# A convolution chain with a Haar shrinkage layer: 25 instead of 21 of 64 final convolutions of three images put off, ScalarE forming 8 instead of 6 of 16 products, and the stores of these convolutions issued from another queue

## The chip, the core and the metric

The kernel runs on one core of one Trainium2 chip. The time is the device time of one execution in microseconds (us). Before the change it was 2994.05 us, the median of three runs (2990.19, 2994.05 and 2999.53). All arithmetic is in 32-bit floating point.

## The reference: what is computed

The input x holds B = 4 images of C = 64 channels, each channel a plane of 256 x 256 numbers. Four layers are applied in sequence.

```python
def conv(x, hx, hy, bias):            # layers 0, 1 and 3, each with its own filter
    k = hx[:, None] * hy[None, :]      # per channel: an outer product of two filters of length 256
    y = irfft2(rfft2(x, 512) * rfft2(k, 512) / 512)[:256, :256]
    return y + x * bias                # a causal 2D convolution plus a skip

def shrinkage(x, v, conv_w, tau):      # layer 2
    f1 = haar2d(x)                     # all levels, along both axes
    for i in range(2):
        f4 = einsum("bchw,oc->bohw", f1 * v[i], conv_w[i])   # channels are mixed
        acc += sign(f4) * relu(abs(f4) - tau[i])
    return haar2d(acc, inverse=True) + x
```

The filters hx and hy come from small networks with sines, computed once per layer. Because a filter is an outer product, the convolution of one plane is two products with triangular Toeplitz matrices, one for the rows and one for the columns.

## The kernel before: how the work is tiled and staged

**One convolution of one plane** is two calls of `contract` (lines 187 to 190), named `first` and `second`. A contract is four matmuls of TensorE: the plane's tile is the stationary operand, a Toeplitz tile `t` read from the padded filter is the moving one, with 256 columns on line 189 and 128 columns on line 190. The result comes out transposed, so two contracts restore the layout. After the first, ScalarE copies the result from PSUM to SBUF (line 198, tile `a`); after the second, VectorE adds the skip (line 211, tile `y`). In a profile the PSUM results are `pa` and `py`. Every fp32 matmul stands there as two records.

**The stages.** Layers 0 and 1 of a batch element run in `convolutions(b)`, which goes on to the Haar transform of the rows and columns (tiles `sd`, `sp`, `pz`, `co`) and stores `keep` and `coef` in DRAM. Then `mixing(b)` takes 64 groups g: four matmuls per group (line 334, result `px`, 128 x 1024 in two PSUM banks, two such results at a time), the product with `v` (lines 351 and 353), absolute value and sign on ScalarE (359, 360), the threshold and the signed product on VectorE (361, 366) and a sum into `z` (370). The 16 strips of 64 columns of the product with `v` are divided: VectorE does 16 - n_act of them in one instruction (line 351), ScalarE does n_act of them in n_act instructions (line 353), which wait for VectorE's. At last `inverse(b)` takes the 64 channels: per channel a strided copy of `z` (387), the inverse Haar along the rows (`pw`, 394 and 395), a rounded part and a remainder (397, 398), the columns (`pu`, 407), three VectorE instructions that form the plane `u` (411, 414, 415), and then layer 3's convolution of that plane and its store (`last`, lines 430 to 435).

**What is put off.** Mixing of image b runs beside the convolutions of image b + 1. The last mixing, of image 3, has none beside it. So layer 3's convolutions of some channels of images 0, 1 and 2 (`put_off`, line 455: the channels 2, 5, ..., 62, 21 of 64) are not done in `inverse`: the plane `u` is stored in DRAM (`late`, line 425) and is loaded again during the last mixing by `convolution` (lines 437 to 448), which spreads all 63 of them evenly over that mixing's ticks. Each of these loads a plane (`v`, tag "in", three buffers), loads a Toeplitz tile (tag "toep", five buffers), and runs `first`, `second` and the store of the result (tag "co", two buffers).

**Order.** Every stage is entered in a list with a tick and a place (`at`), the list is sorted, and the program is built in that order (lines 488 and 489); the compiler then arranges the instructions of each engine, still in one fixed order per engine, by costs of its own. Each engine works through its list in order and waits where a semaphore asks it to. A DMA issued by SyncE or by ScalarE likewise stands in that engine's list. `spread` (line 451) gives the ticks: 63 convolutions over 71 ticks, so at most one begins in a tick.

Of the kernel before, what the change touches and what calls it, by code (L numbers as in the profile page):

```python
# [16 lines left out]
B, C, S, EMB, ORD = 4, 64, 256, 33, 64  # L17
P = 128
# [19 lines left out]
def conv_seq_kernel(ctx, tc, x, fz, fw, bias, decay, haar, haar_row, factors, vt, taut, wmix, out):  # L38
# [14 lines left out]
    nc = tc.nc  # L53
# [123 lines left out]
    def toeplitz(layer, c, name):  # L177

        t = tp.tile([P, 2, S], F32, name=name, tag="toep")
        nc.sync.dma_start(t, ap(pads[layer], c * 2 * ROW, [[1, P], [ROW, 2], [1, S]]))  # L180
        return t
# [34 lines left out]
    def butterfly(b):  # L216

        d = mx.tile([P, 2, C], F32, name=f"bfly_{b}", tag="mag")
        nc.vector.tensor_sub(d, z[:, :, 0, :], z[:, :, 1, :])
        nc.vector.tensor_add(z[:, :, 0, :], z[:, :, 0, :], z[:, :, 1, :])  # L220
        nc.vector.tensor_copy(z[:, :, 1, :], d)
# [5 lines left out]
    def at(tick, place, run, unit):  # L227
        events.append((tick, place, len(events), run, unit))
# [81 lines left out]
    def mixing(b, start, n_act):  # L310

        st = {}

        def load(g):
            f = mx.tile([P, 2, S], F32, name=f"f_{b}_{g}", tag="f", bufs=3)
            nc.sync.dma_start(f, coef[b].rearrange("k c p w -> (k c) p w")[:, 2 * g : 2 * g + 2])
            st[g] = {"f": f}
            if g % GT == 0:
                t = mx.tile([P, 2, GT, 16], F32, name=f"vt_{b}_{g}", tag="vt")
                nc.sync.dma_start(t, scales[g // GT])  # L320
                st["vt", g // GT] = t

        def scale(g, i):
            return st["vt", g // GT][:, i, g % GT, :]

        def over(g, i, n):
            return scale(g, i)[:, :n].unsqueeze(2).to_broadcast([P, n, C])

        def mix(g):
            f = st[g]["f"]  # L330
            ps = psx.tile([P, 2, 2, S], F32, name=f"px_{b}_{g}", tag="mix")
            for q in range(2):
                for h in range(2):
                    nc.tensor.matmul(  # L334
                        ps[:, h, q, :],
                        f[:, q, h * P : (h + 1) * P],
                        wb.rearrange("p r n -> p (r n)"),
                        start=True,
                        stop=True,
                    )  # L340
            if g == 0:

                one, two = ps[:, :, 0, :P], ps[:, :, 0, P:]
                d = mx.tile([P, 2, P], F32, name=f"d_{b}", tag="mag")
                nc.vector.tensor_copy(d, two)
                nc.vector.tensor_sub(two, one, d)
                nc.vector.tensor_add(one, one, d)
            f4 = mx.tile([P, 16, C], F32, name=f"f4_{b}_{g}", tag="f4")
            px = ps.rearrange("p h q (r i o) -> p (h q r i) o", r=2, i=2)
            n = 16 - n_act  # L350
            nc.vector.tensor_tensor(f4[:, :n], px[:, :n], over(g, 0, n), ALU.mult)  # L351
            for j in range(n, 16):
                nc.scalar.mul(f4[:, j], px[:, j], scale(g, 0)[:, j : j + 1])  # L353
            st[g]["f4"] = f4

        def shrink(g):
            f4 = st[g]["f4"]
            mag = mx.tile([P, 16, C], F32, name=f"mag_{b}_{g}", tag="mag")
            nc.scalar.activation(mag, f4, AF.Abs)  # L359
            nc.scalar.activation(f4, f4, AF.Sign)  # L360
            nc.vector.tensor_sub(mag, mag, over(g, 1, 16))  # L361
            st[g]["mag"] = mag

        def signed(g):
            mag = st[g]["mag"]
            nc.vector.scalar_tensor_tensor(mag, mag, 0.0, st[g]["f4"], ALU.max, ALU.mult)  # L366

        def add(g):
            parts = st.pop(g)["mag"].rearrange("p (h r i) o -> p h r i o", h=2, i=2)
            nc.vector.tensor_add(z[:, :, 4 * g : 4 * g + 4, :], parts[:, :, :, 0, :], parts[:, :, :, 1, :])  # L370

        for g in range(S // 4):
            at(start + g - 2, 0, load, g)
            for s, stage in enumerate([mix, shrink, signed, add]):
                at(start + g + s, -1 - s, stage, g)

    def inverse(b, start, put_off):

        st = {}

        def fetch(c):
            if c == 0:
                butterfly(b)
            r = mx.tile([P, 2, 2, P], F32, name=f"r_{b}_{c}", tag="f", bufs=3)
            nc.sync.dma_start(r, keep[b][c])
            a = mx.tile([P, 2, 2, P], F32, name=f"zc_{b}_{c}", tag="mag")
            nc.scalar.copy(a, z[:, :, :, c].rearrange("p h (i k) -> p h k i", k=2))  # L387
            st[c] = {"r": r, "z": a}

        def rows(c):  # L390
            a = st[c]["z"]
            ps = psm.tile([P, 2, 2, P], F32, name=f"pw_{b}_{c}", tag="mm")
            for m in range(2):
                nc.tensor.matmul(ps[:, m, 0, :], a[:, 0, m, :], hsinv, start=True, stop=True)  # L394
                nc.tensor.transpose(ps[:, m, 1, :], a[:, 1, m, :], ident)  # L395
            w = mx.tile([P, 2, 2, 2, P], F32R, name=f"w_{b}_{c}", tag="f4")
            nc.scalar.copy(w[:, 0], ps)  # L397
            nc.vector.tensor_tensor(w[:, 1], ps, w[:, 0].bitcast(F32), ALU.subtract)
            st[c]["w"] = w
            if c not in put_off:  # L400
                st[c][2] = toeplitz(2, c, f"t2_{b}_{c}")

        def cols(c):
            ps = psm.tile([P, 2, 2, P], F32, name=f"pu_{b}_{c}", tag="mm")
            flat = "p m e w -> p (m e w)"
            for i in range(2):
                nc.tensor.matmul(  # L407
                    ps.rearrange(flat), hb, st[c]["w"][:, i].rearrange(flat), start=(i == 0), stop=(i == 1)
                )
            t = io.tile([P, 2, 2, P], F32, name=f"t_{b}_{c}", tag="res", bufs=BUFS["res"])  # L410
            nc.vector.scalar_tensor_tensor(t, st[c]["r"], 0.5, ps, ALU.mult, ALU.add)  # L411
            u = io.tile([P, 2, S], F32, name=f"u_{b}_{c}", tag="y", bufs=BUFS["y"])
            v = u.rearrange("p m (w e) -> p m w e", e=2)
            nc.vector.tensor_add(v[:, :, :, 0], t[:, :, 0, :], t[:, :, 1, :])
            nc.vector.tensor_sub(v[:, :, :, 1], t[:, :, 0, :], t[:, :, 1, :])
            st[c]["u"] = u

        ends = last(b, st)
        for c in range(C):

            at(start + c, -1, fetch, c)
            at(start + c + 1, -9, rows, c)
            at(start + c + 2, -8, cols, c)
            if c in put_off:
                at(start + c + 3, -5, lambda c: nc.scalar.dma_start(late[b, c], st.pop(c)["u"]), c)
            else:
                for s, stage in enumerate(ends):
                    at(start + c + 3 + s, s - 7, stage, c)

    def last(b, st):  # L430
        return [
            first(b, st, "u", 2, "a3"),
            second(b, st, "a3", 2, "u", "y3", "co"),
            lambda c: nc.scalar.dma_start(out[b, c].rearrange("(k p) w -> p k w", p=P), st.pop(c)["y3"]),
        ]

    def convolution(which, ticks):

        for (b, c), tick in zip(which, ticks):
            st = {}  # L440

            def load(c, b=b, st=st):
                u = io.tile([P, 2, S], F32, name=f"v_{b}_{c}", tag="in", bufs=3)
                nc.sync.dma_start(u, late[b, c])
                st[c] = {"u": u, 2: toeplitz(2, c, f"t2_{b}_{c}")}

            for s, stage in enumerate([load, *last(b, st)]):
                at(tick + s, -s, stage, c)


# [1 line left out]
        return [begin + i * (end - begin - 1) // (n - 1) for i in range(n)]  # L452


    put_off = range(2, C, 3)

    one, two, three = filters(0, nc.scalar), filters(1, nc.scalar), filters(2, nc.sync)
    one[0]()
# [14 lines left out]
    ahead = C  # L473
    start = ready + 3
    for b in range(B):
        mixing(b, start, 12 if b + 1 < B else 6)
        end = start + groups + 3
        if b + 1 < B:
            ready = convolutions(b + 1, spread(ahead, end + 2), in_parts=range(0, C, 2 if b == 0 else 1), border=end)
        else:  # L480
            convolution(
                [(i, c) for i in range(B - 1) for c in sorted(put_off)], spread(start - 2, end + 2, (B - 1) * len(put_off))
            )
        inverse(b, end, put_off if b + 1 < B else ())

        start = max(end + C, ready + 3)
        ahead = start - 3
# [111 lines left out]
```

## Time and profile before

| What | Value |
|---|---|
| median of three runs | 2994.05 us |
| the profiled execution, its own time | 2994.63 us |
| its span, first to last instruction | 2992.8 us |
| TensorE clock granted | 1.000 of full |
| TensorE matmul busy | 2929.2 us, 98% of the span |
| TensorE weight loads busy | 2610.1 us, 87% |
| VectorE busy | 2535.0 us, 85% |
| ScalarE busy | 2147.1 us, 72% |
| DMA, read and written in HBM | 426.77 MB and 219.48 MB |

The stages follow from the first and the last `px` matmul of each mixing, in microseconds from the start of the span:

| Stage | from | to | length |
|---|---|---|---|
| filters, tables, layers 0 and 1 of image 0 | 0 | 457.5 | 457.5 |
| mixing 0 / inverse 0 | 457.5 / 867.4 | 867.4 / 1099.7 | 409.9 / 232.3 |
| mixing 1 / inverse 1 | 1099.7 / 1543.0 | 1543.0 / 1779.4 | 443.3 / 236.4 |
| mixing 2 / inverse 2 | 1779.4 / 2222.3 | 2222.3 / 2455.75 | 442.9 / 233.45 |
| mixing 3 / inverse 3 | 2455.75 / 2728.5 | 2728.5 / 2992.8 | 272.75 / 264.3 |

An engine's busy time is the union of the times of its instructions. A mean duration of an instruction is longer than the distance from its start to the next start where instructions overlap, so where work is added up below, distances of starts are used. PE is TensorE's matmul, PEld its weight load, DVE is VectorE, ACT is ScalarE, SP is SyncE.

### The profile page before, as it was taken

The numbers are of one execution on the slowest core, as the hardware profiler recorded it, in microseconds if no ns is written. First come the engines' busy times: TensorE is split into PE (matmuls) and PEld (weight loads), VectorE is DVE, ScalarE is ACT, GpSimd is POOL, SyncE is SP. The second block draws the span as 40 slices with busy tenths as digits, with TensorE's granted clock in tenths as the row PEclk, the third lists the DMA queues.
The fourth block names the chain that finished last, engine by engine and source line by source line (L and its number), as shares of the span: only waits on it lengthen the run. The fifth ranks groups of instructions, "written<-read, shape, count | busy, mean of one in ns | idle before, by whom it ended". The sixth has DMA issues, their size and how long they took to land. (4 is left out here: it accounts for less than half of the span.)

```text
span 2992.8 us, 51867 instructions
## 1 busy us (share of the span) xinstructions
PE 2929.2 (98%) x16950; PEld 2610.1 (87%) x16950; DVE 2535.0 (85%) x4544; ACT 2147.1 (72%) x4973; POOL 0.2 (0%) x4
## 2 busy tenths in 40 slices
PE   7999999999999999999999999999999999999999
PEld 6899988888888888888888988888888988888998
DVE  4766778999988879999989879999998889998776
ACT  1333337989876658889886658989886768887554
POOL 0000000000000000000000000000000000000000
PEclk9999999999999999999999999999999999999999
DMA  5877776676667876666677876676677887777776
GB/s 146 250 233 230 229 232 207 206 206 199 204 196 245 247 216 202 206 210 201 207 212 241 253 222 198 209 212 202 205 210 234 254 239 229 229 233 220 211 212 186
DMA packets 562496, 649.72 MB, mean 217 GB/s; under 512 B 44369, under 2 KB 447412, under 8 KB 562100
## 3 DMA queue, kind: packets, MB, share of 16 engines
q1 hardware_dynamic: 446132, 494.94, 57.9%
q10 hardware_dynamic: 116096, 151.46, 14.1%
q8 instruction: 137, 2.24, 0.3%
q14 instruction: 131, 1.07, 0.1%
HBM read 426.77 MB, written 219.48 MB: 216 GB/s over the span
## 5 line engine op out<-in xcount | busy, mean ns | idle before, releaser
L189 PE MATMUL py<-t,a 128*128 128x256 f32 x3072 | 923.1, 382 | 19.2 <-ACT a L198 12.3
L198 ACT COPY a<-pa 128x512 f32<-128x512 f32 x768 | 472.4, 617 | 440.6 <-PE pa L190 305.7
L190 PEld LDWEIGHTS py<-t,a 128*128 128x128 f32 x3072 | 583.4, 190 | 79.3
L353 ACT ACTIVATE f<-px,vt 128x64 f32<-128x64 f32 x2688 | 588.8, 351 | 87.7 <-DVE f L351 81.8
L190 PE MATMUL py<-t,a 128*128 128x128 f32 x3072 | 590.1, 274 | 0.0
L189 PEld LDWEIGHTS py<-t,a 128*128 128x128 f32 x3072 | 491.0, 191 | 78.2 <-ACT a L198 35.7
L334 PE MATMUL px<-wb,f 128*128 128x256 f32 x2048 | 503.5, 381 | 16.7 <-ACT f L353 16.7
L334 PEld LDWEIGHTS px<-wb,f 128*128 128x128 f32 x2048 | 362.6, 191 | 62.1 <-ACT f L353 26.7
L361 DVE TENSOR_TENSOR mag<-mag,vt 128x1024 f32<-128x1024 f32 x256 | 312.2, 1220 | 30.9 <-ACT mag L359 28.8
L366 DVE SCALAR_TENSOR_TENSOR mag<-mag,f 128x1024 f32<-128x1024 f32 x256 | 311.9, 1218 | 3.8 <-DVE sd L267 0.3
L397 ACT CAST w<-pw 128x512 fp32r<-128x512 f32 x256 | 150.4, 587 | 227.9 <-PE pw L395 215.1
L189 PE MATMUL pa<-t,y 128*128 128x256 f32 x1024 | 306.9, 382 | 1.7 <-DVE y L211 1.4
L189 PE MATMUL pa<-t,x 128*128 128x256 f32 x1024 | 305.6, 380 | 1.3 <-issue 1.3
L359 ACT ACTIVATE mag<-f 128x1024 f32<-128x1024 f32 x256 | 284.3, 1110 | 18.7 <-DVE z L370 6.8
L387 ACT COPY zc<-z 128x512 f32<-128x512 f32 x256 | 282.4, 1103 | 2.0 <-ACT w L397 0.8
L360 ACT ACTIVATE f<-f 128x1024 f32<-128x1024 f32 x256 | 274.0, 1070 | 12.1 <-DVE sd L266 5.9
L211 DVE SCALAR_TENSOR_TENSOR y<-x,bsb,py 128x512 f32<-128x512 f32 x256 | 190.3, 743 | 57.8 <-PE py L190 49.9
L189 PE MATMUL pa<-t,u 128*128 128x256 f32 x772 | 232.8, 383 | 3.2 <-PE pu L407 3.2
L411 DVE SCALAR_TENSOR_TENSOR t<-r,pu 128x512 f32<-128x512 f32 x256 | 175.1, 684 | 64.1 <-PE pu L407 60.6
L278 DVE TENSOR_TENSOR sp<-sd,sp 128x512 fp32r<-128x512 f32 x224 | 153.9, 687 | 83.0 <-ACT sp L277 81.3
L190 PEld LDWEIGHTS pa<-t,x 128*128 128x128 f32 x1024 | 194.6, 190 | 26.3
L190 PEld LDWEIGHTS pa<-t,y 128*128 128x128 f32 x1024 | 194.5, 190 | 26.3
(67 smaller groups left out, 4449.0 us busy)
## 6 DMA issues: line engine op xcount, KB each, us to landing
t<-pad SPq DMA_DIRECT2D x768, 256.0 KB, 4.0
x<-in_x SPq DMA_DIRECT2D x256, 256.0 KB, 3.9
keep<-sd ACTq DMA_DIRECT2D x256, 256.0 KB, 3.0
coef<-co SPq DMA_DIRECT2D x256, 256.0 KB, 3.2
f<-coef SPq DMA_DIRECT2D x256, 256.0 KB, 4.0
r<-keep SPq DMA_DIRECT2D x256, 256.0 KB, 3.3
out_y<-y ACTq DMA_DIRECT2D x256, 256.0 KB, 3.7
late<-u ACTq DMA_DIRECT2D x63, 256.0 KB, 2.7
```

What stands on the lines that cost most here:

```text
L189: nc.tensor.matmul(ps[:, m, :], src[:, 0, m * P : (m + 1) * P], t[:, ::-1], start=True, stop=False)
L190: nc.tensor.matmul(ps[:, m, P:], src[:, 1, m * P : (m + 1) * P], t[:, : P - 1 : -1], start=False, stop=True)
L198: nc.scalar.copy(a, ps)
L211: nc.vector.scalar_tensor_tensor(y, s[res], bsb[:, layer, c : c + 1], ps, ALU.mult, ALU.add)
L334: nc.tensor.matmul(ps[:, h, q, :], f[:, q, h * P : (h + 1) * P], wb.rearrange("p r n -> p (r n)"), start=True, stop=True,)
L353: nc.scalar.mul(f4[:, j], px[:, j], scale(g, 0)[:, j : j + 1])
L359: nc.scalar.activation(mag, f4, AF.Abs)
L360: nc.scalar.activation(f4, f4, AF.Sign)
L361: nc.vector.tensor_sub(mag, mag, over(g, 1, 16))
L366: nc.vector.scalar_tensor_tensor(mag, mag, 0.0, st[g]["f4"], ALU.max, ALU.mult)
L387: nc.scalar.copy(a, z[:, :, :, c].rearrange("p h (i k) -> p h k i", k=2))
L411: nc.vector.scalar_tensor_tensor(t, st[c]["r"], 0.5, ps, ALU.mult, ALU.add)
```

## The change

Three things change together. `put_off` becomes the channels c with c mod 5 equal to 2 or 4: 25 of 64, 75 in the three images instead of 63. They are spread over the same 71 ticks, so that in four ticks two begin. In the last mixing n_act is 8 instead of 6, so that VectorE's instruction has 512 columns instead of 640 and ScalarE has eight strips instead of six. The stores of the put-off convolutions' results are issued by SyncE instead of ScalarE; the stores of all other results stay on ScalarE.

```diff
-        ends = last(b, st)
+        ends = last(b, st, nc.scalar)
...
-    def last(b, st):
+    def last(b, st, queue):
         return [
             first(b, st, "u", 2, "a3"),
             second(b, st, "a3", 2, "u", "y3", "co"),
-            lambda c: nc.scalar.dma_start(out[b, c].rearrange("(k p) w -> p k w", p=P), st.pop(c)["y3"]),
+            lambda c: queue.dma_start(out[b, c].rearrange("(k p) w -> p k w", p=P), st.pop(c)["y3"]),
         ]
...
-            for s, stage in enumerate([load, *last(b, st)]):
+            for s, stage in enumerate([load, *last(b, st, nc.sync)]):
                 at(tick + s, -s, stage, c)
...
-    put_off = range(2, C, 3)
+    put_off = [c for c in range(C) if c % 5 in (2, 4)]
...
-        mixing(b, start, 12 if b + 1 < B else 6)
+        mixing(b, start, 12 if b + 1 < B else 8)
```

## The prediction

> **What bounds the kernel now.** I read the windows by stage first (the table of stages, from the first and last `px`), then the timeline of a saturated stretch for the pace of each matmul, then the groups and the waits of the last mixing, because that is where the moved work goes. The windows' columns are stretch, length, busy time and count of PE, PEld, DVE, ACT and POOL, granted clock, DMA share and GB/s; the rows are mixing 1, mixing 3, inverse 1 and inverse 2.
>
> ```profile
> 1099.70:1543.00 443.30, 434.92 (x2422) 386.76 (x2420) 408.52 (x713) 387.98 (x1091) 0.00 (x0) 1.00 0.68 206
> 2455.75:2728.50 272.75, 267.96 (x1436) 235.98 (x1435) 265.65 (x311) 233.98 (x553) 0.00 (x0) 1.00 0.79 232
> 1543.00:1779.40 236.40, 234.04 (x1470) 210.88 (x1470) 199.17 (x393) 156.09 (x234) 0.00 (x0) 1.00 0.78 238
> 2222.30:2455.75 233.45, 230.46 (x1445) 207.40 (x1445) 198.47 (x392) 155.50 (x232) 0.00 (x0) 1.00 0.78 239
> ```
>
> TensorE is at 98 to 99% in all of them. In mixing 3 VectorE stands beside it at 265.65 of 272.75 us (97%; 92% in mixing 1), ScalarE at 86% (88%).
>
> Busy time hides small stretches, so I take the pace from starts. In the timeline of the last inverse the engine never waits:
>
> ```profile
> 2802.08 0.39 PE L394 MATMUL pw<-hrow,zc 128*128 128x128 f32 x2
> ...
> 2803.21 0.59 PE L189 MATMUL pa<-t,u 128*128 128x256 f32 x2
> ...
> 2804.51 0.60 PE L189 MATMUL py<-t,a 128*128 128x256 f32 x2
> ...
> 2805.82 0.39 PE L394 MATMUL pw<-hrow,zc 128*128 128x128 f32 x2
> ```
>
> A channel's `pw` and `pu` take 1.13 us, a contract 1.31 (2803.21 to 2804.51, and to 2805.82), a convolution 2.62. The four `px` of a group take 1.73 (eight records from 2602.95 to 2604.68).
>
> With these, mixing 3 is 64 x 1.73 = 110.7 us, plus 115 contracts (460 records of line 189, four each) x 1.31 = 150.7, plus 0.5 for a `pu`: 261.9 of work in 272.75. So **10.8 us are lost, 4.1% of the work**. Mixing 1: 226 contracts 296.1, `px` 110.7, 49 split `pz` at 0.47 (0.55 from start to start, less 0.08 by which the record before is shorter) 23.0, `pu` 0.5: 430.3 of 443.3, lost 13.0 or 3.0%. Mixing 2 has the same work in 442.9: 2.9%.
>
> Who is late in mixing 3, from the waits in that stretch (total, times, longest):
>
> ```profile
> ACT f L353 <- DVE f L351: 14.5, 18, 1.8
> PEld px L334 <- ACT f L353: 6.7, 12, 1.2
> PEld py L189 <- ACT a L198: 5.8, 17, 0.8
> DVE y L211 <- DMA out_y<-y: 1.6, 2, 0.9
> ```
>
> The chain is VectorE's part of the product with `v`, then ScalarE's, then `px` gets its banks back. VectorE at 97% starts it.
>
> **What the Trainium skill says.** "Perfetto Trace Analysis", section "Identifying the Most-Contended Engine", warns that matmul busy time is no measure of the distance to the limit, and names the weight loads' share. The trace agrees: matmul 98% in both, weight loads 86.5% in mixing 3, but 203.06 of 220 us (92%) in the stretch of the last inverse without waits. "ScalarE: Activation LUTs", section "What ACT_TABLE_LOAD costs", gives about 280 ns + 0.833 ns per column for an activation with one operand per partition, 333 ns at 64 columns as an estimate, with overlap back to back. The row of line 353 shows 326 ns, and six end after 1.33 us, so a further one costs (1.33 - 0.33) / 5 = 0.20; I use 0.20. "DMA: Bandwidth & Descriptors", section "Issuing engines are not separate DMA queues": another issuer saves only issue time. The trace shows that time on ScalarE's queue as 0.42 us (2612.45), inside a sign instruction that runs from 2612.14 to 2613.20.
>
> **The change, part by part.**
>
> *Twelve more convolutions put off.* Nothing is saved: 12 x 2.62 = 31.4 us of TensorE move. The order of the changed program, which is fixed once it is built, has 8, 8 and 6 contracts fewer between the mixings (22 x 1.31 = 28.8 us), 20 more from the first `px` to the last in mixing 3 (26.2) and 2 more behind it (2.6). The sum is zero, so the result hangs on lost time alone. The extra 12 stores and 12 loads of 256 KB use DMA: mixing 3 moves per group 272 KB for `px` and now 75/70 x 768 KB for convolutions, 1.10 MB in about 4.6 us, 240 GB/s; the page shows slices of 253 and 254 without such waits, so I take zero.
>
> *In the three inverses* per channel remain 1.13 us and 2 x 0.6 contracts instead of 2 x 0.667. VectorE loses only eight `y` (each 0.66 from start to start) there: in inverse 1 it goes from 199.2 of 236.4 us (84%) to about 193.9 of 225.9 (86%). TensorE stays the bound. I add 0.3 us to each for less slack, 1 in all; bounds are -1 (less to wait for) and +2 each.
>
> *Eight products instead of six* in mixing 3. VectorE: line 351 takes 818 ns at 640 columns and 420 at 256 (the row of mixing 0), 1.04 ns per column, so 128 fewer save 0.13 us per group. Its distances of starts in one group (from line 351 at 2604.27: 0.73, 1.14, 0.60, 1.14 behind it, and 0.66 per `y`) make 3.61 + 0.9 x 0.66 = 4.20 us now, and 3.48 + 1.07 x 0.66 = 4.19 after. ScalarE: six strips to the absolute value 1.41, that 0.97, copy 0.46, sign 0.96 (2609.30 on) make about 3.75; after, 1.81 + 0.97 + 0.96 + 1.07 x 0.46 = 4.23. TensorE: from 261.9 / 64 = 4.09 to 1.73 + 135 x 1.31 / 64 = 4.50. So VectorE, at 4.20 in a group of 4.26 now, comes to 4.19 under a TensorE of 4.50 (93%), ScalarE to 94%.
>
> *Stores from SyncE.* Removed from ScalarE: no busy time, as above. Added to SyncE: 75 issues of 0.38 us, in a queue with some 1.3 us of issues per group. The new wait, for `y`, has the next loads behind it. In the changed order the store of convolution k stands directly ahead of the `v` load of k + 3, whose buffer (three of them) is freed by that same `y`, so it waits no longer than before; then come `f` and `t`, used one or more groups later. With a landing of 3.7 to 4.0 us that hides. If that cover goes, in the four ticks with two convolutions, it costs up to 1.5 us each. The two waits for `out_y` (1.6 us on VectorE) may go; worth nothing while TensorE is the bound. Bounds: -1.6 and +6; value 0.
>
> **The sum.** Mixing 3 after: 110.7 + 135 x 1.31 + 0.5 = 288.1 us of work. Its balance is then that of mixing 1 (VectorE 93, ScalarE 94 against 92 and 88), so I take mixing 1's loss, 3.0%: 8.6, in all 296.7, +23.9. Inverses -28.8 + 1.0, last inverse +2.6. Total -1.3 us. Behind the last `px` five convolutions follow each other in both orders, and TensorE waits for the copy in each (2731.52, 2735.08, 2738.64: 3.56 apart instead of 2.62), so that loss stays. The profiled execution, 2994.63 (span 2992.8 and 1.8 around it), becomes 2993.3; the median of the runs lies 0.6 below it: **2993 us**.
>
> **The rivals.**
>
> *Faster.* VectorE's pressure is the whole loss, and once it has slack mixing 3 loses 0.5%, 1.4 us: 288.1 + 1.4 - 272.75 - 28.8 + 2.6 = -9.4, 2985 or below. For it: the longest chain of waits begins at VectorE. Against: mixings 1 and 2, with VectorE at 92%, still lose 3%.
>
> *A new wait on SyncE's queue.* The stores hold back loads in the four double ticks, +6 us: 2999. For it: `v` has one conv's slack less there. Against: no wait of TensorE for a load stands among those of mixing 3 now.
>
> *Slower: the copy comes late.* With ScalarE at 94%, `a` (line 198), which stands between `pa` and `py`, is queued behind eight strips or an absolute value. From the end of `pa` (2734.24) to `py` (2735.08) an undelayed copy takes 0.84 us; two `px` between them cover 0.87, three 1.30. In the changed order 17 of 60 such gaps hold two, against 9 of 54, and 27 hold three against 22. Delays beyond 0.03 us in the former and 0.46 in the latter reach TensorE: 0.4 us in each of the 44 is 18 us, plus the 2 to 3 that remain otherwise, 20 (7%) where 10.8 were: +9 on -26.2 + 26.2, and with 1 to 2 in the inverses 3005. It decides once ScalarE's group passes TensorE's 4.50, that is above 0.23 us per strip. Against: trains of 12 in mixing 1 run while it loses 3%.
>
> **How the numbers follow.** My forecast 0.55, the SyncE wait 0.07, faster 0.12, slower 0.26. A measurement of this kernel tells about 0.3% (9 us) from no change, so the first two count as the same: 0.62. Range: low from a loss of 1.5% in mixing 3 (-4.3) and 1 us less in each inverse (-4), with the stores' 1.6: 2983; high from a loss of 8% (+14) and 1 us in each inverse (3 instead of the 1 that I took, +2): 3009. It leaves the ends of the outer cases out.
>
> **What would show it.** Mixing 3 about 297 us, the inverses 222, 226 and 226; VectorE below 94% and ScalarE at 91 to 94% of mixing 3; waits of `px` for line 353 smaller, of `py` for line 198 about as now. I am wrong if mixing 3 passes 303 us with `py` waiting for the copy over 12 us, or if the inverses shorten by less than 7 us each.

## The result and the profile after

| | median | range | ratio to the kernel before, 95% |
|---|---|---|---|
| before | 2994.06 us | 2990.19 to 2999.53, 20 runs | |
| after | 2999.82 us | 2995.23 to 3003.28, 20 runs | 1.0020 [1.0014, 1.0027] |

The change costs 5.8 us, where I forecast a gain of 1.3. That is inside the 0.3% that I had called about no change; with twenty runs on each side the interval excludes it. The profiled execution of after took 3002.87 us (span 3001.1), 3 us above its median; the one of before had a span of 2992.8, so the two traces differ by 8.3.

| stage | before | after | forecast | difference to forecast |
|---|---|---|---|---|
| head | 457.5 | 458.8 | 457.5 | +1.3 |
| mixings 0, 1, 2 | 409.9, 443.3, 442.9 | 409.6, 443.4, 443.3 | the same | +0.2 |
| inverses 0, 1, 2 | 232.3, 236.4, 233.5 | 224.2, 228.1, 227.2 | 27.8 less in all | +5.1 |
| mixing 3 | 272.8 | 298.8 | 296.7 | +2.1 |
| last inverse | 264.3 | 267.8 | 2.6 more | +0.9 |

The head's 1.3 says nothing: in traces of kernels with the same head it lies between 455.9 and 461. The inverses gave back 22.7 us instead of 27.8, and mixing 3 grew by 26.0 instead of 23.9. With the forecast's -1.3 the traces miss it by 9.6 us: 5.1 in the three inverses, 2.1 in mixing 3, 0.9 in the last inverse, and the rest in the head and the other mixings.

The windows of after, in the columns and the order of the prediction (stretch, length, busy time and count of PE, PEld, DVE, ACT, POOL, clock, DMA share, GB/s; mixing 1, mixing 3, inverse 1, inverse 2):

```profile
1092.52:1535.96 443.44, 435.43 (x2422) 386.79 (x2420) 408.75 (x713) 387.19 (x1091) 0.00 (x0) 1.00 0.69 206
2434.57:2733.33 298.76, 297.85 (x1596) 255.33 (x1595) 275.64 (x324) 263.77 (x697) 0.00 (x0) 1.00 0.79 241
1535.96:1764.11 228.15, 224.03 (x1406) 201.03 (x1406) 195.58 (x389) 155.22 (x230) 0.00 (x0) 1.00 0.80 242
2207.38:2434.57 227.19, 222.89 (x1398) 199.90 (x1398) 195.68 (x389) 155.11 (x230) 0.00 (x0) 1.00 0.79 241
```

In mixing 3 TensorE is 99.7% busy, against 98.2% before. Read alone, that says the stage is perfect. But its work by starts is 288.1 us, so 10.7 of 298.8 are lost, as many as the 10.8 before. The weight loads' share hints at it: 85.5% (86.5% before), where a stretch without waits had 92%. VectorE fell from 97 to 92%, as forecast; ScalarE is at 88%, not 91 to 94.

The pace of the matmuls has not changed. From the timeline of after in the last inverse (start, duration), a channel from `pw` to `pw` is 3.74 us: 1.13, 1.30 and 1.31.

```profile
2802.80 0.39 PE L394 MATMUL pw<-hrow,zc 128*128 128x128 f32 x2
...
2803.93 0.59 PE L189 MATMUL pa<-t,u 128*128 128x256 f32 x2
...
2805.23 0.60 PE L189 MATMUL py<-t,a 128*128 128x256 f32 x2
...
2806.54 0.39 PE L394 MATMUL pw<-hrow,zc 128*128 128x128 f32 x2
```

Who waits in mixing 3 of after (total us, times, longest):

```profile
ACT a L198 <- PE pa L190: 21.6, 14, 3.8
PEld py L189 <- ACT a L198: 14.2, 55, 0.8
ACT f L353 <- DVE f L351: 11.9, 7, 2.9
...
PEld px L334 <- ACT f L353: 4.8, 12, 0.6
...
DVE y L211 <- DMA out_y<-y: 3.0, 2, 2.5
...
PEld pa L189 <- DMA v<-late: 0.4, 1, 0.4
```

ScalarE waited for VectorE before (14.5); now it waits longest for TensorE's `pa`, and TensorE's `py` waits for ScalarE's copy, 55 times instead of 17. Loads of planes, which would show a blocked SyncE queue, cost 0.4 us on the weight loads. Against the matmuls' usual distances TensorE loses 4.4 us behind those late weight loads of `py`, 3.2 between two `px`, 2.4 between a `px` and a `py`. In the trace of before the same count gives 1.6 behind late weight loads of `py`, 2.6 between two `px`, 1.8 between a `px` and a `py`, and 5.1 between a `pa` and a `px`. So the wait for the `px` banks, which the prediction blamed, did shrink (from 7.7 to 3.2 us), and the wait for the copy grew by as much (from 3.4 to 6.8).

### The profile page after: what moved, and what is told of

It is laid out like the page before. It is cut to its first block, busy times and chain, and to the rows that moved or that the text cites. A ratio compares the mean times of both kernels' runs of the same rounds, so it can differ in the third digit from the quotient of the medians.

```text
span 3001.1 us, 51988 instructions
## 1 busy us (share of the span) xinstructions
PE 2935.7 (98%) x16950; PEld 2605.3 (87%) x16950; DVE 2533.6 (84%) x4544; ACT 2169.3 (72%) x5101; POOL 0.2 (0%) x4
## 5 line engine op out<-in xcount | busy, mean ns | idle before, releaser
L353 ACT ACTIVATE f<-px,vt 128x64 f32<-128x64 f32 x2816 | 615.6, 352 | 83.0 <-DVE f L351 82.6
L359 ACT ACTIVATE mag<-f 128x1024 f32<-128x1024 f32 x256 | 287.7, 1124 | 10.7 <-DVE f L351 6.4
L189 PE MATMUL pa<-t,u 128*128 128x256 f32 x724 | 218.6, 384 | 6.3 <-PE pu L407 5.0
```

What stands on the lines that cost most here:

```text
L189: nc.tensor.matmul(ps[:, m, :], src[:, 0, m * P : (m + 1) * P], t[:, ::-1], start=True, stop=False)
```

## The experiments

**Theories.** *Order*: the change makes the compiler lay out other instruction lists, and in mixing 3 the lists of TensorE and ScalarE fit each other worse, whatever the queue of the stores costs by itself. *Queue*: SyncE's stores hold back the loads behind them. *Copy*: ScalarE with eight strips is simply too full. For the inverses: *held buffer* (a put-off plane's `u`, tag "y" with three buffers, can't be reused until its store has landed) against *cover* (too little TensorE work per channel for VectorE's chain).

### Each edit alone, and two of the three

```diff
# put25_only: on the kernel before
+    put_off = [c for c in range(C) if c % 5 in (2, 4)]
# act8_only: on the kernel before
+        mixing(b, start, 12 if b + 1 < B else 8)
# sync_only: on the kernel before, with `last` taking its queue as in the change
+            for s, stage in enumerate([load, *last(b, st, nc.sync)]):
# after_act_queue: on the kernel after
-            for s, stage in enumerate([load, *last(b, st, nc.sync)]):
+            for s, stage in enumerate([load, *last(b, st, nc.scalar)]):
```

> Only the 25 of 64 channels are put off; six strips on ScalarE, stores on ScalarE as before. If the loss comes from the inverses (cover theory: less TensorE work per channel over VectorE's chain), the three inverses come to about 224, 228 and 227 us as in the changed kernel, and the time is 3000 or more: mixing 3 has VectorE at about 4.32 us per group under TensorE's 4.50, so its loss is 10 to 14 us and its length 298 to 302. If the loss came from the eight strips or the queue of the stores, the inverses would be 222, 226 and 226 and the time 2992 to 2995.

> Only eight strips instead of six in the last mixing, 21 channels put off. Cover theory: the inverses stay at 232, 236 and 233 us; mixing 3 falls from 272.75 by 2 to 4 us, since VectorE gets 0.13 us per group back and 10.8 us are lost there; time 2990 to 2992. Rival (ScalarE with eight strips delays the copy between pa and py): mixing 3 gets 2 us longer or more, time 2996 or above.

> Only the stores of the put-off convolutions go to the sync engine. All theories but one: no change, 2994 within 2 us, mixing 3 at 272 to 273. If stores on the sync queue hold loads back, mixing 3 gets 2 to 6 us longer with waits of pa for v.

> The changed kernel, but with its put-off stores issued by ScalarE. Cover theory: the same as the changed kernel, 3000 within 2 us, inverses 224, 228 and 227. If the stores' queue matters in the last mixing, the difference to 3000 is over 3 us, either way.

| | median | ratio | mixing 3 | inverses 0, 1, 2 |
|---|---|---|---|---|
| put25_only | 3000.82 | 1.0025 [1.0015, 1.0036] | 296.0 | 224.8, 228.2, 229.1 |
| act8_only | 3011.65 | 1.0063 [1.0049, 1.0076] | 287.7 | 232.1, 236.3, 232.1 |
| sync_only | 2999.99 | 1.0018 [1.0011, 1.0025] | 277.9 | 232.3, 236.0, 232.0 |
| after_act_queue | 2997.67 | 1.0013 [1.0006, 1.0019] | 292.6 | 224.6, 229.0, 226.0 |

Every edit alone costs, and the parts don't add: 6.3, 17.2 and 5.5 us by medians alone, 5.8 together. The shortfall of the inverses comes with the 25 planes and with nothing else. In mixing 3 eight strips are worst where they stand alone. The waits of act8_only there:

```profile
PEld px L334 <- ACT f L353: 20.6, 16, 2.7
...
PE px L334 <- ACT f L353: 15.6, 7, 2.3
```

Seven waits of some 2.2 us: at seven places TensorE's list asks for a `px` whose banks ScalarE has not yet read. VectorE had been relieved, and the stage got longer. Not all of it is waiting. The granted clock of this stretch was 0.97, and in all five runs that of the whole execution was 0.997 or 0.998; the trace has five stretches of 3.4 us at half clock, each beginning within 0.7 us of the end of one of the seven waits:

```profile
2537.58 1.69 PE L334 MATMUL px<-wb,f 128*128 128x256 f32 x4 [2.22 <-ACT f L353]
2539.07 1.06 PE L189 MATMUL py<-t,a 128*128 128x256 f32 x2
...
2541.53 0.60 PE L189 MATMUL pa<-t,v 128*128 128x256 f32 x2
```

The pair of matmuls that takes 0.60 us elsewhere took 1.06. Of 27.2 us lost in this stage (287.7 less 260.5 of work) 15.6 are the seven waits, and about 8.5 (half of five times 3.4) are the slower clock. So the 17.2 us hold both.

sync_only has another sort of place: in nine convolutions `py` follows its `pa` directly, with nothing in between to cover the copy.

```profile
PE py L189 <- ACT a L198: 7.1, 14, 0.7
```

The edit only names another queue, yet mixing 3 is 5.2 us longer, and the lists of TensorE, ScalarE and VectorE are others: the kernel before has no such adjacent pair in this stretch. That speaks for *order*, and I pinned orders next.

### TensorE's order alone

A pinned kernel adds dependencies without semaphores between successive instructions of one engine, which fix their order; the traces show the lists in the order given.

```diff
+    for earlier, later in zip(queue, queue[1:]):   # TensorE's matmuls of the last mixing
+        tc.add_manual_dep(later, earlier.name, <no semaphore>)
```

> The changed kernel, stores on the sync queue, but TensorE's order from the first to the last px of the last mixing is pinned to the order that the compiler chose when ScalarE issued the stores (45 gaps between pa and py with four px, instead of 27 with three and 14 with two). Order theory (the queue acts only through the order that the compiler picks): mixing 3 at 292 to 294 us, py waits for its copy a few times instead of 55, time 2996 to 2998. Queue theory (the stores on the sync queue themselves delay something): mixing 3 stays at 298 to 299 and the time at 2999 to 3001.

> The kernel before, stores on ScalarE, with TensorE's order in the last mixing pinned to the one that the compiler chose with the stores on the sync queue (nine gaps between pa and py with nothing in them). Order theory: nine waits of 0.84 us for the copy, mixing 3 at 277 to 279 us, time 2998 to 3001. Queue theory: mixing 3 at 272 to 274, time 2994 to 2995.

after_pinned: 3001.23 us, 1.0021 [1.0014, 1.0029], mixing 3 295.5. before_pinned: 3008.05, 1.0044 [1.0031, 1.0056], mixing 3 286.4 instead of the 277.9 of the kernel whose order it took. Neither settled it. TensorE's list is only half of a pair: with ScalarE's list left as the compiler made it, `py` of before_pinned waited 25.4 us for copies (32 times, on the weight loads).

### All three engines' orders: the queue and the order apart

Now the lists of TensorE, ScalarE and VectorE in mixing 3 (254, 315 and 323 steps) are held to those of after_act_queue, with the stores on SyncE; and then the converse.

```diff
+    for order in ORDERS:               # TensorE, ScalarE, VectorE
+        ...
+            tc.add_manual_dep(later, earlier.name, <no semaphore>)
```

> The changed kernel, stores on SyncE, but with the order of TensorE, ScalarE and VectorE in the last mixing held to that of the version whose stores are on ScalarE's queue, 254, 315 and 323 steps; only the queue of the stores then differs from that version. If the queue matters only through the orders that the compiler made from it: last mixing 292 to 294 us, and about 2997.7. If waits in SyncE's queue, or later loads, are the cost: last mixing 297 to 300, and about 3000 or more.

> The converse: stores on ScalarE's queue, but the three engines' orders in the last mixing held to the changed kernel's. If the order is the cause and the queue is not: last mixing near or above the changed kernel's 298.8 us (299 to 302), about 3002. If the queue has a part of its own that is worth more than 3 us: last mixing 292 to 296, about 2998.

In each field stand mixing 3, its sum with the last inverse, and the median of the whole kernel. The sum is the fairer one, since after's order has 135 contracts ahead of the last `px` and the other 134 (1596 and 1588 records, eight to a contract), with the odd one done behind it.

| | stores on SyncE | stores on ScalarE |
|---|---|---|
| after's order | 298.8; 566.5; 2999.82 | 303.3; 569.4; 3005.73 |
| after_act_queue's order | 289.7; 558.2; 2993.50 | 292.6; 562.9; 2997.67 |

The pinned ones have ratios of 0.9996 [0.9988, 1.0004] (after_all_pinned) and 1.0040 [1.0028, 1.0053]. Down the columns, by the sums, after's order costs 8.3 and 6.5 us (6.3 and 8.1 by medians). Along the rows SyncE's queue *gains* 2.9 and 4.7 (5.9 and 4.2). In each row and each column one kernel is pinned and the other has the compiler's own lists. What pinning does by itself was not run; it enters with opposite signs, so that it drops out of the means, if it adds the same everywhere: 7.4 us for the order and 3.8 for the queue. The change lost the queue's gain to the lists that came with it. This settles *queue* against *order*: both kernels of a column have the same queue.

The window and the waits of mixing 3 of after_all_pinned, where the added lines have moved the numbers (line 353 is 415, 351 is 413, 198 is 255, 189 is 244, 334 is 394, 359 is 422, 360 is 423):

```profile
2433.64:2723.34 289.70, 288.62 (x1588) 258.16 (x1586) 269.46 (x322) 259.96 (x696) 0.00 (x0) 1.00 0.80 247
```

```profile
ACT f L415 <- DVE f L413: 24.1, 56, 2.3
DVE y L270 <- PE py L246: 6.4, 8, 1.6
ACT a L255 <- PE pa L246: 5.9, 4, 3.8
...
PEld px L394 <- ACT f L415: 3.4, 8, 0.6
...
PEld py L244 <- ACT a L255: 0.8, 1, 0.8
```

`py` waits once instead of 55 times. ScalarE's wait for VectorE has doubled, 24.1 us, and costs TensorE next to nothing, since it stands where TensorE has other work: the stage loses 2.9 us in all. The weight loads are at 89.1%, and on 286.8 us of work (134 contracts) the stage loses 2.9, 1.0%. That speaks against *copy* too: the same eight strips per group, with ScalarE busy for 89.7% of the stage, need not cost more.

The two orders, seen in ScalarE's timeline. First after:

```profile
2616.76 1.06 ACT L360 ACTIVATE f<-f 128x1024 f32<-128x1024 f32 x1
2619.17 0.59 ACT L198 COPY a<-pa 128x512 f32<-128x512 f32 x1 [1.36 <-PE pa L190]
2619.66 1.75 ACT L353 ACTIVATE f<-px,vt 128x64 f32<-128x64 f32 x8
```

Then after_all_pinned, one group of it:

```profile
2617.28 0.31 ACT L415 ACTIVATE f<-px,vt 128x64 f32<-128x64 f32 x1 [0.87 <-DVE f L413]
2617.49 1.05 ACT L423 ACTIVATE f<-f 128x1024 f32<-128x1024 f32 x1
2618.43 1.53 ACT L415 ACTIVATE f<-px,vt 128x64 f32<-128x64 f32 x7
2619.81 0.63 ACT L255 COPY a<-pa 128x512 f32<-128x512 f32 x1
```

In after the copy stands ahead of the eight strips here: ScalarE waits 1.36 us for a `pa` that TensorE reaches only after a `px`, and the strips, which free the `px` banks, come late. In the pinned list 57 of the 64 groups have the same turn, first strip, sign of the group before, seven strips, copy; in 45 of the 66 gaps between a `pa` and its `py` four `px` stand, 1.73 us of cover for a copy that takes 0.84. In after's lists 15 groups have that turn, in 14 the copy stands directly ahead of eight strips, and of 67 gaps 14 hold two `px` and no more (0.87) and 27 hold three (1.30).

### The inverses: is the buffer held?

The trace of after shows one such event in inverse 2. VectorE waits 1.17 us for the landing of the store of a put-off plane, and TensorE stands before `pa` for 1.12:

```profile
2412.29 0.43 DVE L414 TENSOR_TENSOR u<-t 128x256 f32<-128x256 f32 x1 [1.17 <-DMA late<-u]
...
2413.15 0.67 PE L189 MATMUL pa<-t,u 128*128 128x256 f32 x2 [1.12 <-issue]
```

no_plane_stores leaves out the stores of the put-off planes, and the last mixing loads stored row coefficients (`keep`) in their place, so that it convolves other data with the same work. gpsimd_half is after_act_queue with one of the two instructions that form `u` on GpSimd, the remedy of *cover*.

```diff
# no_plane_stores
-                at(start + c + 3, -5, lambda c: nc.scalar.dma_start(late[b, c], st.pop(c)["u"]), c)
+                at(start + c + 3, -5, lambda c: st.pop(c), c)
# gpsimd_half
-            nc.vector.tensor_sub(v[:, :, :, 1], t[:, :, 0, :], t[:, :, 1, :])
+            nc.gpsimd.tensor_sub(v[:, :, :, 1], t[:, :, 0, :], t[:, :, 1, :])
```

> The changed kernel without the stores of the put-off planes: their convolutions load the stored differences of the same channel instead, so the output is not the reference's. Landing theory (a plane's buffer, one of three, is held until its store has landed): the loss in the three inverses falls by 1.5 to 2.5 us each, to 222, 226 and 225 us, and the time to 2994 to 2996. Cover theory (TensorE's ticks are shorter than VectorE's chain from pu to the plane): the inverses stay within 0.7 us of 224.2, 228.1 and 227.2 and the time at 2999 to 3001.

> The changed kernel with its stores on ScalarE, and one of VectorE's five instructions per channel in the inverses (the second half of the plane, line 415) on GpSimd. Cover theory: VectorE's chain from pu to the plane gets shorter, if GpSimd takes under about 1 us for 128 x 256 numbers; the loss in the first three inverses falls by 2 us or more each and the time from 2997.7 to 2990 to 2993. If GpSimd takes over 1.2 us, the plane comes later and the inverses get longer: 3000 and more, the last one too. Landing theory: no change but that.

no_plane_stores: 2992.98 us, 0.9992 [0.9984, 1.0000], inverses 223.1, 225.8, 224.6, 6.0 less than after in all. gpsimd_half: 3008.5, 1.0052 [1.0038, 1.0065], inverses 228.8, 231.4, 231.2, 11.8 more than after_act_queue's. The second says nothing on *cover*, because the remedy itself made the plane late. Its group on GpSimd (busy us, mean ns) shows 776 ns, where VectorE needs 420; and in inverse 1 TensorE's `pa` waited for it:

```profile
L415 POOL TENSOR_TENSOR u<-t 128x256 f32<-128x256 f32 x256 | 198.8, 776 | 2797.7 <-DVE t L411 1451.8 <-issue 783.1 <-DVE sd L266 475.7
```

```profile
PEld pa L189 <- POOL u L415: 7.1, 7, 1.8
```

The same question without leaving work out: put-off planes go into buffers that stand idle in an inverse.

```diff
-            u = io.tile([P, 2, S], F32, name=f"u_{b}_{c}", tag="y", bufs=BUFS["y"])
+            tag = "in" if c in put_off and c < 56 else "y"
+            u = io.tile([P, 2, S], F32, name=f"u_{b}_{c}", tag=tag, bufs=3)
```

> The changed kernel, with the plane u of a put-off channel (channels below 56) placed in the buffers of tag in, which stand idle in an inverse, instead of tag y; the work and every transfer remain, and TensorE's order is the same. If a put-off plane's buffer, held until its store has landed, is what kept the inverses long: inverses 223, 226 and 225 us instead of 224.2, 228.1 and 227.2, as with the stores left out, some 5 us in all, and about 2995. If the traffic of the stores itself lengthens them, or ScalarE's time for issuing them: inverses as in the changed kernel within 1 us each, and about 3000.

> The same placement in the version with 25 of 64 put off, eight products on ScalarE and all stores on ScalarE's queue (2997.7 us before). If the held buffer is the cause: some 5 us shorter in the inverses, last mixing 292 to 293 us, about 2992 to 2993, below the kernel before. If not: 2997 to 2998.

> The same placement in the kernel before, where 21 planes per image are stored. If the held buffer costs by the plane: 21/25 of the saving of the changed kernel, some 4 us, inverses 231, 235 and 232 instead of 232.3, 236.4 and 233.5, about 2990. If the buffers became short only with 25 planes (two put-off channels three and two apart instead of three): no difference, 2994 to 2995.

| | median | ratio | inverses 0, 1, 2 | against the same without the edit |
|---|---|---|---|---|
| after_in | 2998.60 | 1.0012 [1.0004, 1.0020] | 222.8, 229.0, 226.4 | -1.3 |
| act_queue_in | 2992.58 | 0.9994 [0.9986, 1.0002] | 221.1, 227.8, 226.6 | -4.1 |
| before_in | 2992.56 | 0.9992 [0.9984, 1.0000] | 230.9, 235.4, 231.1 | -4.8 |

Single traces differ by this much. With the lists of before in the inverses, the three sum to 702.1 us in before, but to 700.3 in sync_only and 700.5 in act8_only; with those of after, to 679.5 in after, 679.6 in after_act_queue and 681.0 in after_all_pinned. Against the means of these traces the other buffers gain 3.0 us in the changed kernels (678.2, 675.5, and 677.3 in all_pinned_in below) and 3.6 in the kernel before (697.4). They came with another list as well: VectorE's differs in 7 to 12 places of each inverse (a `y` stands elsewhere), and it was not held, so the gain belongs to buffer and list together. Since the kernel before gains as much, the held buffer doesn't explain what after lost against before. My theory fell by half: with the planes elsewhere the inverses of act_queue_in are 21.9 us shorter than those of before_in, and the work moved out is 28.8.

### The rest of the inverses, and both remedies together

no_u takes act_queue_in and leaves out, for the put-off channels below 56, the two VectorE instructions that form `u`; `t` is stored in its place. pairs_21 takes before_in and puts the same number of channels, 21, in pairs two apart. all_pinned_in joins the pinned order with the other buffers. pinned_21 tries the good order on 21 planes: twelve convolutions are struck out of it, and in three places two convolutions that it interleaves stand one behind the other.

```diff
# no_u
+            if short:
+                st[c]["u"] = t.rearrange("p m e w -> p m (e w)")
+                return
# pairs_21
-    put_off = range(2, C, 3)
+    put_off = [c for c in range(C) if c % 6 in (2, 4)]
```

> The version with stores on ScalarE and put-off planes in the idle buffers (inverses 221.1, 227.8 and 226.6 us), in which the put-off channels below 56 leave out the two VectorE instructions that form u and store t instead: 0.84 us less VectorE work for each of 22 channels per inverse. If bursts of VectorE's work, at put-off channels that have only 1.13 us of TensorE work, are what still delays the planes and so TensorE: inverses about 219, 223 and 222, 10 us or more in all, and about 2983. If VectorE is not behind these waits: inverses within 1 us each of those without this edit, and about 2992.

> The kernel before with the put-off planes in the idle buffers (inverses 230.9, 235.4 and 231.1 us), and with its 21 put-off channels in pairs two apart (c mod 6 equal to 2 or 4) instead of every third; the number of convolutions moved is the same, 21 per image. If it is the neighbourhood, put-off channels two apart, that makes the inverses of the changed kernel lose 2 to 3 us more than those with every third channel: inverses about 2 us longer each, 233, 237.5 and 233. If it is the number put off (less TensorE work over which an inverse's fixed waits are spread) or the shares of the engines: inverses within 1 us of those without this edit.

> The changed kernel with both edits that helped: the three engines' orders in the last mixing held to those of the version with its stores on ScalarE, and the put-off planes below channel 56 in the idle buffers of tag in. If the two causes are separate and add up: last mixing 290 us, inverses 223, 228 and 226, about 2990. If the buffers only moved the waits: inverses as in the pinned version (223.5, 229.5, 228.0), and 2993 to 2994.

> 21 of 64 put off as in the kernel before, with eight products on ScalarE, the stores on SyncE, the put-off planes in the idle buffers, and the three engines' orders in the last mixing held to the order above with twelve convolutions struck out of it. If the order of the last mixing is what costs and this one is good whatever the number: last mixing 265 to 268 us (work 261.9, loss 1.3 to 2.3%) instead of 272.8, inverses as in the kernel before with that placement (231, 235, 231), about 2984 to 2987. If the lower share of convolutions itself leaves VectorE the bound: last mixing 272 to 274, about 2992.

no_u: 2992.50 us, 0.9995 [0.9987, 1.0004], inverses 222.6, 226.2, 226.4: 0.3 us less in all where 10 were expected. So too much VectorE work at the put-off channels is not the cause, within what such traces differ by.

pairs_21: 2997.74 us, 1.0006 [0.9998, 1.0014], inverses 230.8, 237.9, 236.5. Against before_in that is -0.1, +2.5 and +5.4, with the same number moved. The neighbourhood counts in two of three. TensorE in inverse 1 of pairs_21:

```profile
1637.78 0.71 PE L407 MATMUL pu<-w,hb 128*128 128x512 f32 x2
1639.44 0.67 PE L189 MATMUL pa<-t,u 128*128 128x256 f32 x2 [0.95 <-PE pu L407]
```

And VectorE beside it:

```profile
1636.12 0.69 DVE L278 TENSOR_TENSOR sp<-sd,sp 128x512 fp32r<-128x512 f32 x1 [0.64 <-ACT sp L277]
1636.73 0.68 DVE L398 TENSOR_TENSOR w<-pw,w 128x512 fp32r<-128x512 f32 x1
1637.33 0.68 DVE L411 SCALAR_TENSOR_TENSOR t<-r,pu 128x512 f32<-128x512 f32 x1
1637.93 0.74 DVE L211 SCALAR_TENSOR_TENSOR y<-u,bsb,py 128x512 f32<-128x512 f32 x1
1638.59 0.42 DVE L415 TENSOR_TENSOR u<-t 128x256 f32<-128x256 f32 x1
1638.92 0.42 DVE L416 TENSOR_TENSOR u<-t 128x256 f32<-128x256 f32 x1
```

`u` is formed in VectorE's list behind a `y` and two remainders, and TensorE, with a put-off channel on either side, has no other contract to do until then. By distances of starts inverse 1 of pairs_21 has three stalls of 1.12 to 1.14 us of this form, before_in none above 0.60. The changed kernel has one in inverse 1 (1640.44) and one in inverse 2 (2311.30), also with the buffers moved: about 2 us of its loss. The neighbourhood alone does not make a stall: of the twelve such pairs in an inverse of the changed kernel at most one stalls so. The remaining stalls are shorter ones of several sorts, among them `pw` waiting 0.5 to 1.3 us for the copy `co`, whose buffer waits for the landing of an `out_y`. I didn't separate them; that part stays open.

all_pinned_in: **2989.03 us** (2987.00 to 2994.44, 21 runs), 0.9987 [0.9981, 0.9994], faster than both kernels. Mixing 3 289.8, inverses 223.1, 228.4, 225.8: 3.7 less than pinned alone (223.5, 229.5, 228.0). The two remedies add up.

pinned_21: 3016.21 us, 1.0078 [1.0065, 1.0091], mixing 3 293.3 where I expected 265 to 268. A miss. An order with convolutions struck out is no longer a good one:

```profile
PEld px L392 <- ACT f L413: 29.7, 27, 1.6
ACT f L413 <- DVE f L411: 22.0, 34, 5.0
PE px L392 <- ACT f L413: 19.5, 23, 1.2
```

Where a convolution is missing, the next `px` comes sooner than ScalarE's turn of strips. This order did not carry over to another proportion of work; whether 21 planes have one as good is not shown.

## Why the prediction was wrong

*Work moved.* Right: 8, 8 and 6 contracts fewer, 20 and 2 more, at 1.31 us each, and the sum zero. Everything hung on lost time, as said. Two terms of lost time failed: the inverses' 0.3 us each, and the 0 for the stores' queue with the 3.0% taken for mixing 3.

*"I add 0.3 us to each for less slack, 1 in all; bounds are -1 and +2 each."* This step failed in size. The inverses shortened by 8.1, 8.3 and 6.3 of 10.5, 10.5 and 7.9: 6.1 us lost instead of 1, beyond the bounds in two, and the third fell under the 7 us that I had named as a sign of being wrong. I looked at the busy shares of VectorE (84 to 86%; 85.7 measured in inverse 1), and they don't tell a stall at one place. What I hadn't looked at: which channels stand beside each other, and which buffers a put-off plane holds. Runs showed about 2 us for the neighbourhood. The other buffers, with the list that came with them, are worth some 3 us, but before gains as much. So the cause of some 4 of the 6.1 us stays open.

*"The page shows slices of 253 and 254 without such waits, so I take zero"* for stores and loads. Bandwidth was not the matter, in this I was right: mixing 3 of after_all_pinned moves 247 GB/s in the shorter time. Landing was, for buffers that wait for it.

*"Bounds: -1.6 and +6; value 0"* for SyncE. The size reached toward the upper bound: +3.6 in mixing 3 and the last inverse together (562.9 to 566.5), +2.1 by medians, and +5.2 where it stands alone (537.1 to 542.3). The mechanism was another. With the orders held SyncE's queue gains 2.9 to 4.7; what costs is the order of the lists that the compiler built with it. No load was held back (0.4 us), so that the rival of a wait on SyncE's queue, which said 2999, met the number by luck. I had counted how many `px` lie between `pa` and `py` in the order given, and used it only for a rival.

*Mixing 3's loss of 3.0%.* Measured 10.7 us of 288.1, 3.7%; the 2.1 us are the difference. The other queue's order gave 5.8 of 286.8 (2.0%), the same order with SyncE 2.9 (1.0%), the converse 15.2 of 288.1 (5.3%). So there is no loss that belongs to a "balance" of shares, as I took from mixing 1: the same work, split in the same way, lost 1.0 to 5.3%, and that 3.0% came near was luck. So was it that after_all_pinned's 2993.50 us meets the forecast of 2993: its mixing 3 is 7.0 us shorter than forecast, its three inverses are 6.6 us longer.

*The rivals.* "Slower: the copy comes late" named the right place, gaps of two and three `px` and `py` waiting. Its price was too high: 6.8 us of TensorE's time at `py` (4.4 and 2.4) instead of 18; of the 14.2 us by which weight loads of `py` came late less than half reached the matmuls. Its condition was wrong as well: ScalarE is not over its limit (88%). My sum for it was too high: I took 1.81 us for eight strips, and from their start to that of the copy behind them it is 1.56 (2613.57 to 2615.13 in after). "Faster" came near with the better order, 2.9 us of loss in mixing 3 where that rival said 1.4; but what decided was the order, not VectorE's slack: VectorE is busy for 92% of mixing 3 in after and for 93% in after_all_pinned.

## What to carry to other kernels

Where each engine works through one fixed list, an edit can change the lists as well as the work, even one that only names another queue. To judge the edit, hold the lists of all the engines that hand work to each other, not of one, and compare. Before moving work out of a stage, ask which neighbours it leaves and which buffers it holds until a store lands; buffers that stand idle in that stage cost nothing here. A TensorE that is 99.7% busy can still lose 3.7%: add up the work by starts; the weight loads' share (85.5% at 3.7% lost, 89.1% at 1.0%) is a rough sign.

## What was not expected of the hardware

GpSimd took 776 ns for a subtraction of 128 x 256 fp32 that VectorE does in 420, and it formed half of each plane so late that the inverses grew by 2.4 to 5.2 us each. Moving 75 store issues of about 0.4 us off ScalarE, at a held order, made mixing 3 and the last inverse 2.9 to 4.7 us shorter, though ScalarE was at 87 to 90% of that mixing and I had counted those issues at nothing. The prediction took issue time for all that another issuer saves; here more changed. In that mixing the median store landed 3.8 and 3.5 us after its issue from SyncE (after, after_all_pinned), but 4.6 and 4.7 from ScalarE (act_queue_pinned_to_after, after_act_queue), and the Toeplitz loads beside them, always issued by SyncE, took 3.9 and 4.0 against 4.7 and 4.6. Which of the two gave the gain was not taken apart.

In act8_only five of seven waits of 2.2 us on TensorE were followed by 3.4 us at half the clock (from 2538.0, 2579.0, 2654.1, 2695.0 and 2736.0); those that ended at 2498.39 and 2614.86 were not. What decides it is not shown, but a wait of 2.2 us could cost 1.7 more.
